# A four-image metaformer on one core: the scans' carried state multiplied into the factor by GpSimd, side work dealt by other weights, and the last token loads issued from ScalarE

## The chip, the core and the metric

The kernel runs on one core of a Trainium2 chip. The metric is the device time of one execution in microseconds (us). Before the change the median of three runs is 9317.89 us (9309.0 to 9324.41). One further execution was profiled; its own time is 9321.34 us, and its span in the trace is 9319.6 us.

## What is computed

The input x is four images of 64 x 64 tokens with 128 channels. Two layers follow each other, and each adds a mixing part and then a feed-forward part to x. In outline:

```
x  = x + ss2d(norm(x))            # in-projection, 3x3 depthwise convolution, four selective scans,
                                  # norm, gate, out-projection
t  = t + experts(norm(t))         # softmax over the 4096 tokens of an image for each of 64 experts,
                                  # the 8 best tokens of each expert pooled by their probabilities,
                                  # two dense layers, result added back to those tokens
x  = x + row_and_column_sums(norm(x))
t  = t + stu(norm(t))             # long convolutions with 16 filters by Fourier transform
```

The selective scan of the reference, for one image, one of four directions, and each of 256 channels d and 16 states n:

```
dA = exp(dt * A);   h = dA * h + (dt * u) * B;   y = sum over n of h * C     # one after the other over 4096 tokens
```

The expert part in the reference takes the softmax first and then picks its eight largest values:

```
probs = softmax(logits, axis=1); vals, idx = top_k(probs, 8)
pooled = sum(x[idx] * vals);  out = gelu([pooled, 1] @ weight1);  out = [out, 1] @ weight2;  outputs[idx] += out * vals
```

## The kernel before, in words

**The scan loop** (L2340 to L2479) makes up most of the program. An image is worked in 32 chunks: four directions k times eight pieces of 512 tokens. A chunk is worked in 16 steps, one for each state n, with the channels in two halves h of 128 partitions. Four images give 128 chunks and 2048 steps. In a step s the engines do this:

- SP (SyncE) issues the load of B and C for step s+5, spread over all partitions (tile bc, L2347).
- ScalarE computes da = exp(dl * aneg) for step s+3, 128x512 for each half (L2357). There are five da buffers.
- VectorE multiplies db = du * B for each half (L2414); du and db lie in PSUM. Then it runs the scan hh = da * h + db for each half with tensor_tensor_scan (L2420). The scan's initial value is the constant 0 in the first chunk of a direction (step == 0), and in the other seven chunks the state that the chunk before ended with, read from the tile hst: 1792 of the 2048 steps.
- GpSimd copies the last column of hh of step s-1 into hst (L2432, 128x2), and multiplies hh by C in place (L2433, 128x1024).
- TensorE transposes hh of step s-2 and adds it up in PSUM (L2460).

For directions 2 and 3 all of it runs from right to left.

**Waits taken early** (L2420 to L2423). The second scan of step s is given three dependencies ahead of need: on da of step s+1 (the dictionary acts), on GpSimd's multiplication of step s-7 and on TensorE's transposes of step s-7, since there are eight hh buffers (HH = 8).

**Chunk sizes** (step_sizes, L2233): in steps 1 to 10 of a chunk, dl and dx of the next chunk are made in pieces, among them two GpSimd operations of 128x1024 (L2271 and L2280). At step 15 ScalarE copies dx to du in PSUM (into_psum, L2337).

**Side work.** Everything else of the layers runs beside the scans as generators that yield a number after each piece of work, its supposed cost. Twice in each step the function deal takes pieces until their sum has caught up with what is due; what falls due at each call comes from the list WEIGHT (one total for each image, L41). Steps 2, 3 and 14 of a chunk deal nothing (BUSY). Dealt pieces stand in each engine's queue behind that step's own instructions. Helpers of the side work: norm_sums (L350: ScalarE makes sums and squares of four or two 128-wide rows), norm_refine (L369: six small GpSimd operations), norm_apply and transposed, pipelined (runs stages over groups, a cost for each stage).

**The experts of the first three images** (experts_and_sums, L1155) are side work. VectorE takes the maximum of each logit piece (L1197), ScalarE takes the exponentials (L1209) and scales them by one over their sum (L1219), VectorE picks the top eight of the probabilities (L1223) and blanks them (L1226), and GpSimd subtracts, so that only the eight values stay. Pooling and the two dense layers follow. The experts of the last image have their own function.

**After the scans**: the last image's experts and layer 1, then spectrum (L1930): 32 rounds of products on TensorE with copies alternating between VectorE and ScalarE. Its tile wt takes 128 KB of each partition. Each round sends its products to memory (zf), and the next round reads them back, transforms them (backward, L2044) and stores zd. Last comes endings (L2110): eight groups, for each of which zb (from zd) and the tokens x3 (tile xr) are loaded, four pairs of products are made, scaled and added to xr on VectorE (L2141), and xr is stored to out (L2145). All these loads and stores are issued by SP, in the order of the program.

Of the kernel before, what the change touches and what calls it, by code (L numbers as in the profile page):

```python
# [10 lines left out]
F32 = mybir.dt.float32  # L11
# [6 lines left out]
P = 128  # L18
# [22 lines left out]
WEIGHT = (1275.0, 1008.0, 1346.0, 927.0)  # L41
# [6 lines left out]
BP = 64  # L48
# [62 lines left out]
def kernel(  # L111
# [310 lines left out]
    def front(first_sizes):  # L422
# [6 lines left out]
        with tc.tile_pool(name="fr", bufs=2) as fr:  # L429
# [176 lines left out]
            for g in range(1, 8):  # L606
# [15 lines left out]
                for h in range(2):  # L622
                    if g == 1:
                        ps = cv[1][h]
                    else:
                        ps = bank([P, 8, W], "cv_ps")
                        for t in range(0, 9, 3):
                            taps_pe(ps, g, h, range(t, t + 3))
                            yield 2.6
# [57 lines left out]
    def before_scans(b):  # L687
# [6 lines left out]
        with tc.tile_pool(name="pa", bufs=1) as pa:  # L694
            xnT = pa.tile([P, L], F32, name="xnT")
            with tc.tile_pool(name="pa_n", bufs=2) as pn:
# [6 lines left out]
                def sums(g):  # L703
# [5 lines left out]
                    (3.0, sums),  # L709
                    (1.2, lambda g: norm_refine(pn, st[g], 4, C, 1e-6)),  # L710
                    None,
                    (1.2, lambda g: norm_apply(xt[g], xt[g], st[g], 4)),
                    None,
                    (1.0, lambda g: transposed(xnT[:, 512 * g : 512 * (g + 1)], xt[g], 4, "xt_ps")),
                )
            later(3, lambda: nc.sync.dma_start(xn_d[b], xnT))
            with tc.tile_pool(name="pa_c", bufs=2) as pc:
                for h in range(2):
# [17 lines left out]
                    for g in range(8):  # L736
                        ps = bank([P, 8, W], "cv_ps")
                        for t in range(9):
# [8 lines left out]
                            if t % 3 == 2:  # L747
                                yield 2.6
# [60 lines left out]
    def gate(b):  # L809

        z_d[b] = dram.tile([2, P, L], F32, name=f"z_d{b}")
        with tc.tile_pool(name="pa_z", bufs=2) as pz:
# [24 lines left out]
            yield from pipelined(16, (0.5, load), None, None, (2.8, project), (1.3, mul), (0.5, put))  # L837

    def after_scans(b, last=None):

        with ExitStack() as pools:
# [85 lines left out]
            if not last:  # L927
# [3 lines left out]
                    (2.2, add),  # L931
                    (2.0, sums),
                    (1.2, lambda g: norm_refine(po, st[g], 2, DI, 1e-5)),
                    None,
                    (1.2, apply),
                    None,
                    (1.0, turn),
                    (1.2, gated),
                    None,
                    (1.4, project),  # L940
# [65 lines left out]
    def filters():  # L1006

        with tc.tile_pool(name="fl", bufs=2) as fp:
# [45 lines left out]
            for src, acc in ((m_plus, accp), (m_minus, accm), (m_u, mu_t)):  # L1054
                n = src.shape[1]
                for i in range(4):
                    for k in range(0, n, 4):
# [10 lines left out]
                        yield 1.5  # L1068
            for k in range(0, KF, 4):
# [10 lines left out]
                yield 3.0  # L1080
# [11 lines left out]
        with tc.tile_pool(name="hd_w", bufs=2) as hp:  # L1092
# [41 lines left out]
            for q in range(0, NQ, 4):  # L1134
# [18 lines left out]
                yield 2.0  # L1153

    def experts_and_sums(b):  # L1155

        with tc.tile_pool(name="mk", bufs=1) as kp:
            pT = kp.tile([E, L], F32, name="pT")
            outE = kp.tile([E, C], F32, name="outE")
            pooled = kp.tile([P, E], F32, name="pooled")  # L1160
            with tc.tile_pool(name="ga", bufs=2) as gp:
                tt = gp.tile([P, NBLK, C], F32, name="tt", bufs=1)
                mx8 = gp.tile([E, 8], F32, name="mx8", bufs=1)
# [15 lines left out]
                def logits(g):  # L1179
# [7 lines left out]
                    (3.0, sums),  # L1187
                    (1.2, lambda g: norm_refine(gp, st[g], 4, C, 1e-5)),
                    None,
                    (1.2, lambda g: norm_apply(t4(g), t4(g), st[g], 4)),  # L1190
                    None,
                    (1.0, turn),
                    (1.0, logits),
                    None,
                    (
                        0.6,
                        lambda g: nc.vector.reduce_max(  # L1197
                            mx8[:, g : g + 1], pT[:, gs(g)], axis=AX.X
                        ),
                    ),  # L1200
                )
                yield LAG

                nmx = gp.tile([E, 1], F32, name="nmx", bufs=1)
# [1369 lines left out]
```

## Time and profile before

| what | us |
|---|---|
| median of three runs | 9317.89 |
| profiled execution, its time | 9321.34 |
| profiled execution, its span | 9319.6 |
| scan stage: from the first db to the end of the last scan | 48.0 to 7639.9 |
| last image's experts and layer 1 | to about 7877 |
| spectrum, 32 rounds | to about 9174 |
| rest of the last backward, and endings | to 9319.6 |

| engine | busy us | share of the span |
|---|---|---|
| TensorE (PE) | 7286.4 | 78% |
| VectorE (DVE) | 8204.7 | 88% |
| ScalarE (ACT) | 6078.9 | 65% |
| GpSimd (POOL) | 6345.1 | 68% |

GpSimd works almost only in the scan stage: its digits in the table of 40 slices are 6 to 9 until slice 33 and 0 in the last seven. A row of a group in the profile gives line, engine, operation, output and inputs with their shapes and the count; after the first bar the busy time in us and the mean of one in ns; after the second bar the idle time of the engine just before these instructions, with what ended most of it. A row of the waits gives who waited for whom, the sum in us, how often, and the longest. A row of the windows gives each engine's busy time in a stretch of the span, the clock granted to TensorE, the busy share of the DMA engines and their rate.

### The profile page before, as it was taken

What the parts mean: (1) busy time and instruction counts of PE and PEld (TensorE: products, weight loads), DVE (VectorE), ACT (ScalarE), POOL (GpSimd) and SP (SyncE); (2) the same over time, 40 slices, a digit from 0 to 9 for tenths busy, and PEclk for the clock granted to TensorE, in tenths of its full rate; (3) what the DMA queues carried; (4) which work ended last, traced back from release to release, by engine and by line L of the source; (5) the groups of instructions that cost most, each with busy time, mean ns of one, the idle gap of its engine ahead of it and who ended that gap; (6) DMA issues with size and microseconds to landing.
All of it is one profiled execution on the core that took longest, in us unless ns stands there. A gap on an engine that the chain in (4) does not pass through costs nothing.

```text
span 9319.6 us, 139792 instructions
## 1 busy us (share of the span) xinstructions
PE 7286.4 (78%) x45218; PEld 4705.1 (50%) x45218; DVE 8204.7 (88%) x9342; ACT 6078.9 (65%) x11459; POOL 6345.1 (68%) x5833
## 2 busy tenths in 40 slices
PE   7778787577777777787868777768777768999996
PEld 4445454355544555454544554544555445555663
DVE  8999999989999999999999999999999974556663
ACT  6676767657855576776875686875577763555552
POOL 6778788969888788877978798977888870000000
PEclk8889797668778888798878897868888878999998
DMA  5656657658566656657857656856756775333336
GB/s 167 214 194 205 210 185 250 202 187 253 188 201 222 221 174 198 207 185 235 254 178 245 223 174 220 260 171 238 239 179 209 218 224 171 96 90 94 95 95 181
DMA packets 918579, 1806.25 MB, mean 194 GB/s; under 512 B 86593, under 2 KB 476513, under 8 KB 914137
## 3 DMA queue, kind: packets, MB, share of 16 engines
q1 hardware_dynamic: 917848, 1797.30, 60.2%
q8 instruction: 363, 5.95, 0.3%
q14 instruction: 368, 3.01, 0.1%
HBM read 1554.75 MB, written 242.22 MB: 193 GB/s over the span
## 4 chain that ended last, share of the span: by engine, by line
POOL 34%; PE 24%; issue 15%; DVE 10%; ACT 8%; DMA 7%; SPq 1%; POOLq 0%; DVEq 0%; ACTq 0%
POOL hh L2433 26%; PE sp_ps L1944 10%; DVE hh L2420 5%; PE y L2460 4%; DVE wt L1948 3%; ACT da L2357 3%; DVE db L2414 2%; PE dl_ps L2277 2%; POOL hst L2432 2%; DMA bc<-bc_d 2%; POOL dx L2280 2%; POOL ex L2271 1%; DMA yk<-y_d 1%; ACT no_sq L362 1%; PE cv_ps L740 1%
## 5 line engine op out<-in xcount | busy, mean ns | idle before, releaser
L2433 POOL TENSOR_TENSOR hh<-hh,bc 128x1024 f32<-128x1024 f32 x2048 | 4830.9, 2360 | 330.2 <-DVE hh L2420 176.6
L2420 DVE TENSOR_TENSOR_SCAN hh<-da,hst,db 128x512 f32<-128x512 f32 x3584 | 4385.7, 1265 | 112.1 <-PE y L2460 61.7
L2460 PE MATMUL y<-ident,hh 128*128 128x128 f32 x16384 | 2623.4, 314 | 1094.1 <-POOL hh L2433 1005.2
L2357 ACT ACTIVATE da<-dl,aneg 128x512 f32<-128x512 f32 x4096 | 2776.6, 717 | 1054.5 <-DVE hh L2420 1042.2
L2460 PEld LDWEIGHTS y<-ident,hh 128*128 128x128 f32 x16384 | 2198.4, 162 | 1979.4 <-POOL hh L2433 1336.4
L2414 DVE TENSOR_TENSOR db<-du,bc 128x512 f32<-128x512 f32 x4096 | 2618.9, 684 | 151.6 <-ACT du L2337 107.9
L2432 POOL COPY hst<-hh 128x2 f32<-128x2 f32 x1792 | 336.8, 188 | 701.8 <-DVE hh L2420 628.4
L1948 DVE COPY wt<-sp_ps 128x1024 f32<-128x1024 f32 x512 | 606.6, 1221 | 168.6 <-PE sp_ps L1944 146.4
L1944 PE MATMUL sp_ps<-vt,pT_a 32*128 32x256 f32 x8192 | 592.6, 400 | 53.1 <-DVE wt L1948 32.8
L2420 DVE TENSOR_TENSOR_SCAN hh<-da,db 128x512 f32<-128x512 f32 x512 | 596.4, 1206 | 19.3 <-ACT no_r L366 9.9
L1948 ACT COPY wt<-sp_ps 128x1024 f32<-128x1024 f32 x512 | 515.4, 1016 | 121.5 <-PE sp_ps L1944 102.4
L1944 PEld LDWEIGHTS sp_ps<-vt,pT_a 32*128 32x128 f32 x8192 | 394.7, 185 | 246.9 <-DVE wt L1948 190.4
L1948 DVE COPY zs<-sp_ps 128x1024 f32<-128x1024 f32 x132 | 161.7, 1225 | 363.9 <-DMA gq<-dft_out 132.7
L1944 PE MATMUL sp_ps<-wt,ut 128*32 128x256 f32 x8192 | 450.3, 380 | 2.0 <-ACT ut L1948 2.0
L740 PE MATMUL cv_ps<-xh,diag 128*128 128x512 f32 x864 | 398.8, 597 | 4.4 <-ACT sg_v L409 3.1
L2277 PE MATMUL dl_ps<-ex,ident 128*128 128x512 f32 x508 | 308.7, 696 | 118.2 <-POOL ex L2271 113.6
L2252 PE MATMUL dt_ps<-dts,dtw 8*128 8x512 f32 x508 | 351.8, 798 | 49.1 <-ACT sg_v L409 24.1
L1944 PEld LDWEIGHTS sp_ps<-wt,ut 128*32 128x32 f32 x8192 | 263.6, 110 | 197.0 <-issue 25.2
L2280 POOL TENSOR_TENSOR dx<-dl,xc 128x1024 f32<-128x1024 f32 x127 | 300.3, 2365 | 89.9 <-ACT dl L2278 85.6
L2278 ACT COPY dl<-dl_ps 128x512 f32<-128x512 f32 x254 | 147.3, 580 | 324.6 <-PE dl_ps L2277 323.7
L1948 ACT COPY zs<-sp_ps 128x1024 f32<-128x1024 f32 x132 | 133.6, 1012 | 329.5 <-DMA zf<-zs 212.4
L2271 POOL TENSOR_TENSOR ex<-ex,dx 128x1024 f32<-128x1024 f32 x127 | 299.9, 2362 | 49.2 <-ACT dx L2268 40.0
(400 smaller groups left out, 9067.5 us busy)
## 6 DMA issues: line engine op xcount, KB each, us to landing
bc<-bc_d SPq DMA_DIRECT2D x2048, 512.0 KB
xc<-xc_d SPq DMA_DIRECT2D x128, 512.0 KB
y_d<-ys SPq DMA_DIRECT2D x128, 512.0 KB
w1t<-in_w_dram SPq DMA_DIRECT2D x96, 512.0 KB
w2t<-in_w_dram SPq DMA_DIRECT2D x192, 256.0 KB
yk<-y_d SPq DMA_DIRECT2D x128, 256.0 KB
yk<-y_d SPq DMA_DIRECT2D x256, 128.0 KB
zf<-zs SPq DMA_DIRECT2D x512, 64.0 KB
```

The costliest lines, as they stand in the source:

```text
L740: nc.tensor.matmul(ps, diag[:, h, t, :], xh[:, 8 * g + dy : 8 * g + dy + 8, dx : dx + W], start=(t == 0), stop=(t == 8),)
L1944: tc.keep_in_program_order(nc.tensor.matmul(*args, **kw))
L1948: tc.keep_in_program_order(copy(dst, src))
L2271: nc.gpsimd.tensor_sub(ex, ex, dx)
L2277: nc.tensor.matmul(ps, ident, t[:, h], start=t is dl, stop=t is w)
L2280: nc.gpsimd.tensor_mul(dx, dl, xc)
L2357: i_act = nc.scalar.activation(das[t][:, h, :], sizes[t // N][0][:, h, :], AF.Exp, scale=aneg[:, tk, h, t % N : t % N + 1],)
L2414: nc.vector.tensor_mul(db[h], dus[i][h], bcs[s][:, 0, :])
L2420: i_dve = nc.vector.tensor_tensor_scan(o, d0, d1, init, ALU.mult, ALU.add)
L2432: nc.gpsimd.tensor_copy(hsts[t // N][:, :, t % N], hhs[t][:, :, last])
L2433: i_pool = nc.gpsimd.tensor_mul(hhs[t], hhs[t], bcs.pop(t)[:, 1:2, :].to_broadcast([P, 2, SC]))
L2460: i_pe = nc.tensor.matmul(ys[c][:, q, h, :], hhs[t][:, h, q * P : (q + 1) * P], ident, is_transpose=True, start=(n == 0 and k > 0 and q % ...
```

## The change

There are four parts.

**1. The carried state.** In steps of chunks with step > 0, GpSimd multiplies the first-processed column of da by hst before the scan (two values in each partition, 128x2), and the scan starts from the constant 1. The multiplication for step s+2 stands in GpSimd's queue ahead of the copy and the multiplication of step s-1. It takes the place of the exponential in acts, so that the early wait of the second scan of step s is now for GpSimd's multiplication for step s+1.

```
+            t = s + 2
+            if 0 <= t < total and chunks[t // N][2] > 0:
+                col = SC - 1 if chunks[t // N][1] >= 2 else 0
+                d0 = das[t][:, :, col]
+                i_fold = nc.gpsimd.tensor_mul(d0, d0, hsts[t // N - 1][:, :, t % N])
+                acts[t] = i_fold.ins.name
...
-                    init = 0.0 if step == 0 else hsts[i][:, h, n : n + 1]
+                    init = 0.0 if step == 0 else 1.0
```

**2. Side work weighed anew.** The costs that the pieces yield are changed, and with them the totals. No work is added or removed by this; other pieces stand beside other steps.

```
-WEIGHT = (1275.0, 1008.0, 1346.0, 927.0)
+WEIGHT = (1494.0, 1288.0, 1692.0, 1196.0)
...
-                            yield 2.6
+                            yield 3.1
...
-                    (3.0, sums),
-                    (1.2, lambda g: norm_refine(pn, st[g], 4, C, 1e-6)),
+                    (5.4, sums),
+                    (2.2, lambda g: norm_refine(pn, st[g], 4, C, 1e-6)),
...
-                        yield 1.5
+                        yield 2.4
```

The first yield is that of three convolution taps; the last that of the filters (L1068). Nearly all stages of pipelined are changed in this way: those with norm_sums, norm_refine, norm_apply and GpSimd multiplications by factors of 1.2 to 2.3, the projections and expert products hardly or not.

**3. Raw top eight** (the experts of the first three images). The top eight are taken of the logits. The maximum is the first of them, the exponentials stay without their division, and the eight values get the same exponential, so that match_replace finds them. One over the sum is applied to the first dense layer's output, on the way out of PSUM, and to the second's.

```
-                        lambda g: nc.vector.reduce_max(
-                            mx8[:, g : g + 1], pT[:, gs(g)], axis=AX.X
-                        ),
...
+                nc.vector.max(top, pT)
...
-                nc.vector.reduce_max(nmx, mx8, axis=AX.X)
-                nc.vector.tensor_scalar(nmx, nmx, -1.0, None, ALU.mult)
+                nc.vector.tensor_scalar(nmx, top[:, 0:1], -1.0, None, ALU.mult)
...
+                nc.scalar.activation(top, top, AF.Exp, bias=nmx)
-                for g in range(8):
-                    nc.scalar.activation(pT[:, gs(g)], pT[:, gs(g)], AF.Identity, scale=ssum)
-                    yield 0.8
-                nc.vector.max(top, pT)
...
-                evict(h1, hps)
+                nc.scalar.activation(h1, hps, AF.Identity, scale=ssum)
...
+                nc.scalar.activation(outE, outE, AF.Identity, scale=ssum)
```

**4. The endings' tokens.** After the last product of spectrum, its tiles wt and zs and the pool that holds the taps are released, and all 32 token loads are issued on ScalarE's queue, ahead of the last read-back and the last backward. Two of the eight groups take the room of the older pool; the other six and zb take that of zs and wt. The copy of the last backward goes to VectorE. In endings SP issues zb and out alone.

```
+            right.close()
+            last_pool.__exit__(None, None, None)
+            begin_endings()
             load_back(n - 1)
             backward(n - 1)
...
-                out(zo, ps, 1)
+                out(zo, ps, 1 if i + 1 < n else 0)
...
+        for g in range(n):
+            for b in range(B):
+                nc.scalar.dma_start(xr[g][:, b], mine(x3_d, b, g))
...
-            def load_x(g):
-                xr[g] = gp.tile([P, B, 4, C], F32, name="xr3", bufs=6)
-                for b in range(B):
-                    nc.sync.dma_start(xr[g][:, b], mine(x3_d, b, g))
```

## The prediction

> **What bounds the kernel now.** I read the page's busy shares and slices first, then the groups of instructions, then the waits of the scan stage, then windows of the endings.
>
> ```profile
> PE 7286.4 (78%) x45218; PEld 4705.1 (50%) x45218; DVE 8204.7 (88%) x9342; ACT 6078.9 (65%) x11459; POOL 6345.1 (68%) x5833
> ...
> DVE  8999999989999999999999999999999974556663
> ...
> POOL 6778788969888788877978798977888870000000
> ```
>
> The second and third lines are the slices of VectorE and GpSimd. VectorE is at 9 tenths until slice 33, that is, through the whole scan stage of 7592 us (48.0 to 7639.9). The windows view gives VectorE 7304.6 us busy there, 96%, GpSimd 6298.4 us (83%), TensorE 76%, ScalarE 69%. So VectorE sets the pace, and what its instructions save is time, unless it then waits.
>
> ```profile
> L2433 POOL TENSOR_TENSOR hh<-hh,bc 128x1024 f32<-128x1024 f32 x2048 | 4830.9, 2360 | 330.2 <-DVE hh L2420 176.6 <-DMA dts_d<-xd_st 2.4 <-DMA bc<-bc_d 1.7
> L2420 DVE TENSOR_TENSOR_SCAN hh<-da,hst,db 128x512 f32<-128x512 f32 x3584 | 4385.7, 1265 | 112.1 <-PE y L2460 61.7 <-ACT da L2357 14.2 <-ACT vs L295 11.5
> ...
> L2420 DVE TENSOR_TENSOR_SCAN hh<-da,db 128x512 f32<-128x512 f32 x512 | 596.4, 1206 | 19.3 <-ACT no_r L366 9.9 <-ACT da L2357 5.7 <-PE y L2460 1.2
> ...
> L2432 POOL COPY hst<-hh 128x2 f32<-128x2 f32 x1792 | 336.8, 188 | 701.8 <-DVE hh L2420 628.4 <-PE y L2460 10.3 <-DMA bc<-bc_d 9.2
> ...
> L374 POOL TENSOR_TENSOR no_a<-no_a,no_r 128x2 f32<-128x2 f32 (+1 forms) x200 | 39.5, 197 | 31.0 <-ACT no_r L366 20.6
> ...
> L1197 DVE TENSOR_REDUCE mx<-pT 64x1 f32<-64x512 f32 x24 | 15.7, 654 | 0.0
> ```
>
> A step of VectorE is two db (684 ns) and two scans. The scans that read hst take 1265 ns, those with a constant 1206 ns, same shapes. From the records' starts, an undisturbed step lasts 3538 ns with hst and 3417 ns without. The rows behind L2432 and L374 are the price of 128x2 on GpSimd: 188 ns a copy, 197 ns a multiplication.
>
> ```profile
> DVE db L2414 <- ACT du L2337: 107.9, 65, 7.3
> DVE hh L2420 <- PE y L2460: 62.9, 35, 7.2
> ...
> DVE hh L2420 <- ACT da L2357: 20.0, 16, 3.2
> ```
>
> VectorE stands idle some 280 us of the stage. Of that 162 us end with ScalarE (107.9 for du, 20.0 for da, the rest five small rows), 63 us with TensorE's transposes, 40 us with the loads of bc. VectorE hardly ever waits for GpSimd directly today.
>
> **Scans from a constant.** 1792 steps are of the kind with hst. By the row means, 3584 x 59 ns = 211 us; by the step starts, 1792 x 121 ns = 217 us. I take 217: overlaps between instructions are in it, and the 256 steps without hst are the same instruction with a constant already. All of it is on the path.
>
> **The fold on GpSimd.** 1792 x 197 ns = 353 us busy. A GpSimd instruction that needs nothing of the one before starts about 60 ns before that one ends, so the queue grows by some 140 ns a step, 250 us. What hides it is GpSimd's waiting for scans, 805 us (rows hst 628.4 and hh 176.6). That cover is thin: copy 188, a gap of 80, multiplication 2360, less 55 of overlap is 2.57 us a step; side work on GpSimd in the stage is 1228 us, 0.60 a step; with the fold 3.31 us, against 3.42 of an undisturbed step of VectorE and some 3.6 with its idle time. Were the cover gone wholly, up to 250 us would come back; that is within the slower rival below.
>
> Here a rule speaks against the change. The Trainium skill, GPSIMD Engine Reference, section "Performance versus the Vector engine", keeps elementwise work on VectorE, because GpSimd dispatches each instruction through two software hops. The row agrees that it is dear: 197 ns for two columns. By the rule the fold would be VectorE's: with the form (N+151)/0.96 ns of VectorE: DVE Perf Modes (its section on the TRN2 errata) that is 159 ns, an estimate, x 1792 = 285 us on the engine that is the bound, 68 us more than the scans save. By the row it is 353 us on an engine with 805 us of waiting. I take the row; what the rule warns of is paid in the next term.
>
> **The new wait.** The second scan of step s now waits for the fold of s+1. In GpSimd's queue that stands behind the multiplication of s-3, and behind side work dealt in between; and it waits itself for da of s+1, with the copy and multiplication of s-2 queued behind it. Before, VectorE waited for the multiplication of s-7 only. The multiplication ends within 2.7 us of its scan's end in a quarter of the steps, 3.0 in half, 7.5 in 95 of 100, 19.8 at most. The second scan of step s starts 3 x 3.42 - 1.17 = 9.1 us after the scan of s-3 has ended. Less the usual 2.7 and the fold's 0.2, a burst of about 6 us on GpSimd is covered; by the same sum for s-7 some 20 us were.
>
> No trace of before shows the wait, so I count it from the records: where would the fold end, if it followed the multiplication of s-3 and its da, and is that behind the start of the second scan? In 67 of 2044 steps, in 23 bursts; within a burst one delay serves all, and the largest of each add up to 28 us. With a further lag of 1, 1.5, 2 or 3 us the same count gives 58, 78, 101 and 169 us. The lag does grow: in a burst GpSimd loses 0.14 us a step to the fold and 0.12 to the faster VectorE; over six steps 1.6 us. I take the row for 1.5 us, +78 us, with the ends +28 and +169. Below zero it can't go: the fold takes no wait away.
>
> **The weights.** In both programs the pieces of each image add up to its total within 1%, so nothing is left over for an image's end. What changes is the crowding. I sum the side instructions of each engine between the steps in the order of the two programs, each at the mean of its line's row. On GpSimd the largest sum in three consecutive steps falls from 14.9 to 8.7 us. On ScalarE the largest in 16 steps falls from 71.6 to 57.6 us, and the 99th percentile from 61 to 51, where the step's own two exponentials of 717 ns leave some 34 us (16 x (3.6 - 1.43)). The waits of VectorE that end with ScalarE, 162 us, come from such crowds; I take a quarter off, -40 us. Ends: -80 (half), and +20, since the convolution taps stand a few per cent closer than before. TensorE is what comes next there: in the stretches 150 to 430, 660 to 920, 1140 to 1420 and 4040 to 4320 it is 82 to 87% busy.
>
> **Raw top eight.** Row L1197: 24 maxima x 654 ns = 15.7 us leave VectorE, beside scans that follow without a gap: -16 us. MAX8 and MATCH_REPLACE8 (4.39 and 4.40 us each) stay. ScalarE loses 24 scalings of 710 ns (17 us) and gains six small ones; off the path, zero. If ScalarE were late there, it could only help.
>
> **Endings.**
>
> ```profile
> core 0: us, PE busy (x) PEld busy (x) DVE busy (x) ACT busy (x) POOL busy (x), PEclk, DMA share, GB/s
> ...
> 9174.00:9190.00 16.00, 5.81 (x8) 2.21 (x8) 0.00 (x0) 1.42 (x2) 0.00 (x0) 0.79 0.38 119
> 9190.00:9200.00 10.00, 0.00 (x0) 0.00 (x0) 0.00 (x0) 0.00 (x0) 0.00 (x0) 0.60 0.83 179
> 9200.00:9310.00 110.00, 68.29 (x121) 28.16 (x122) 21.78 (x29) 0.00 (x0) 0.00 (x0) 0.79 1.03 266
> ```
>
> After the last product the DMA engines are 38% busy for 16 us and 83% for 10 us, then full to the end. The empty part is 16 x 0.62 + 10 x 0.17 = 11.6 us. SP issues the first token load at 9191.8, behind the wait for zd; ScalarE's last copy ends at 9174.4, and from there it can issue. Everything after is transfer (8 MB each of zb, x3 and out), so filling the hole is worth 11 us. Behind the waiting ScalarE stands nothing; zq, zd and the first zb now share the engines with tokens, and the second half of the first zb waits for half of the token loads, but transfers run meanwhile. VectorE's copy of zo instead of ScalarE's is +0.2 us. Ends: 0 (if the read-back is delayed by as much) and -15.
>
> The rule here: DMA: Bandwidth & Descriptors of the Trainium skill, section "Issuing engines are not separate DMA queues", says that a second issuing engine saves only issue time. The token loads hold SP for 32 us of issuing (eight groups, 2.2 to 6.5 us), but under full DMA engines, so by the rule alone the gain would be nothing. By the windows the start moves 17 us earlier into a hole. I take the windows.
>
> **Sum.** -217 - 16 - 11 + 78 - 40 = -206 us, against the profiled execution's 9321.3: 9115 us. (The median of the runs is 3.4 us lower than that execution; too little to shift it.) The scan stage would take 7592 - 217 - 16 + 78 - 40 = 7397 us.
>
> **Rivals.**
>
> *The bound moves on.* VectorE is 3.4% faster, the others are not. In the four stretches where TensorE is 82 to 87% busy, some 1100 us or 300 steps, 121 ns a step (36 us) are not earned; the fold costs its upper end of 169, the weights bring nothing: 9321 - 244 + 36 + 169 = 9282 us; down to 9200 in milder forms. For it: VectorE's waits for TensorE lie just there. Against: TensorE's granted clock in them is 0.88 to 0.93, not full.
>
> *All of it arrives.* Waits at the lower end of 28, weights at -80: 9321 - 244 + 28 - 80 = 9025 us. For it: the thinner crowds are exactly what makes the fold late. Against: GpSimd at 3.31 of 3.42 us.
>
> *Slower: the fold holds GpSimd behind a late ScalarE.* The fold waits for da in order, ahead of a multiplication that could run. By the records da of s+2 ends after GpSimd could go on in 331 of 2044 steps, in sum 832 us. The gain is used up when 244 / 832 = 29% of that reaches VectorE. At 40% it is 333 - 244 = +89: 9410 us. Against it: in a burst the same lateness is counted in each step, GpSimd has 6 us in hand, and VectorE itself waited for da only 20.0 us in 16 places.
>
> **Chances.** The forecast (9050 to 9200) 0.67; the bound moves on (9200 to 9300) 0.18; all of it arrives (below 9050) 0.07; slower 0.08. A measurement of this kernel can tell about 0.2% (19 us) from no change. Of the second case 0.03 falls within that: faster 0.89, same 0.03, slower 0.08. The range 9050 to 9260 leaves out the third and fourth cases and some 0.04 of the second.
>
> **What would show it.** All 4096 scans at about 1206 ns, none with hst; 1792 multiplications da<-da,hst near 197 ns; a new wait of the scans for POOL da between 28 and 169 us; VectorE's waits ending with ScalarE nearer 120 than 162 us; L1197 gone; DMA engines over 90% busy from the last product on. I am wrong if the scans keep 1265 ns, if waits for POOL da pass 250 us, or if GpSimd's fold row has hundreds of us of idle time ended by ACT da.

## The result and the profile after

The changed kernel takes 9443.61 us (median of three runs, 9437.12 to 9450.17) against 9317.89: it is slower, ratio 1.0136 with a 95% interval of 1.0113 to 1.0159, or +126 us. The prediction of 9115 us was wrong in sign. The profiled execution has a span of 9448.4 us. Its scan stage lasts 7727.6 us (47.7 to 7775.3; before 7591.9), and what follows the stage 1673.1 (before 1679.7). So the loss lies in the scans.

First the busy shares and the slices of VectorE and GpSimd on the page after:

```profile
PE 7331.3 (78%) x45218; PEld 4741.4 (50%) x45218; DVE 7990.5 (85%) x9316; ACT 6070.9 (64%) x11441; POOL 6614.9 (70%) x7625
...
DVE  8898898889999999888989997999998983566553
...
POOL 7788888879988888887988897888888881000000
```

VectorE lost 214 us of work (8204.7 to 7990.5), where the sum had 217 + 16, and GpSimd gained 270. But VectorE's digits, 9 nearly throughout the stage before, are now often 8, in a longer stage: it does less and waits more. The groups of instructions say how much, and for what:

```profile
L2444 POOL TENSOR_TENSOR hh<-hh,bc 128x1024 f32<-128x1024 f32 x2048 | 4834.2, 2361 | 278.8 <-DVE hh L2431 130.4 <-DMA fr<-dft_in 3.2 <-DMA bc<-bc_d 1.3
L2431 DVE TENSOR_TENSOR_SCAN hh<-da,db 128x512 f32<-128x512 f32 x4096 | 4772.2, 1203 | 489.8 <-POOL da L2373 311.8 <-PE y L2471 162.5 <-PE xt_ps L395 5.3
...
L2373 POOL TENSOR_TENSOR da<-da,hst 128x2 f32<-128x2 f32 x1792 | 349.6, 200 | 155.8 <-ACT da L2361 137.8 <-DMA ud<-uo 4.6 <-DMA bc<-bc_d 3.0
...
L2443 POOL COPY hst<-hh 128x2 f32<-128x2 f32 x1792 | 339.7, 190 | 547.6 <-DVE hh L2431 492.4 <-PE y L2471 6.4 <-DMA bc<-bc_d 6.3
```

All 4096 scans take 1203 ns, and a fold takes 200 ns: both as forecast. New is the idle time ahead of the scans, 489.8 us where it was 131, and 311.8 us of it end with the fold (POOL da, L2373). The waits, for the lines that the prediction had shown:

```profile
DVE hh L2431 <- POOL da L2373: 311.8, 209, 5.5
...
DVE hh L2431 <- PE y L2471: 162.5, 65, 16.1
...
POOL da L2373 <- ACT da L2361: 137.8, 92, 5.8
...
DVE db L2425 <- ACT du L2341: 87.5, 35, 6.8
```

In the whole stage VectorE is idle for 638 us, where it was 287: +351. Its work in the stage fell by 215 us (7304.6 to 7089.3). The difference is 136 us, and by that the stage grew.

The endings, by windows that begin where the last product is nearly done:

```profile
9300.00:9310.00 10.00, 8.77 (x164) 5.02 (x156) 3.68 (x3) 3.04 (x3) 0.00 (x0) 1.00 0.41 81
9310.00:9320.00 10.00, 1.71 (x2) 0.84 (x3) 0.00 (x0) 0.00 (x0) 0.00 (x0) 0.67 0.87 271
9320.00:9330.00 10.00, 4.64 (x7) 1.40 (x5) 1.23 (x1) 0.00 (x0) 0.00 (x0) 0.67 0.85 264
9330.00:9340.00 10.00, 0.00 (x0) 0.00 (x0) 0.00 (x0) 0.00 (x0) 0.00 (x0) 0.50 0.83 252
9340.00:9350.00 10.00, 0.00 (x0) 0.00 (x0) 0.00 (x0) 0.00 (x0) 0.00 (x0) 0.50 1.01 238
```

The DMA engines (last but one column) stand at 0.83 to 0.87 right after the last product, where they were at 0.38 before. The hole is filled.

### The profile page after: what moved, and what is told of

Same layout as the page of the kernel before. It is cut to its first block, busy times and chain, and to the rows that moved or that the text cites. A ratio compares the mean times of both kernels' runs of the same rounds, so it can differ in the third digit from the quotient of the medians.

```text
span 9448.4 us, 141374 instructions
## 1 busy us (share of the span) xinstructions
PE 7331.3 (78%) x45218; PEld 4741.4 (50%) x45218; DVE 7990.5 (85%) x9316; ACT 6070.9 (64%) x11441; POOL 6614.9 (70%) x7625
## 4 chain that ended last, share of the span: by engine, by line
POOL 38%; PE 24%; issue 14%; DVE 8%; DMA 8%; ACT 7%; SPq 0%; POOLq 0%; DVEq 0%; ACTq 0%
POOL hh L2444 26%; PE sp_ps L1934 10%; PE y L2471 4%; DVE hh L2431 3%; DVE wt L1938 3%; DMA bc<-bc_d 3%; PE dl_ps L2281 2%; ACT da L2361 2%; POOL da L2373 2%; POOL hst L2443 2%; POOL ex L2275 2%; POOL dx L2284 2%; DVE db L2425 2%; PE cv_ps L740 1%; PE dt_ps L2256 1%
## 5 line engine op out<-in xcount | busy, mean ns | idle before, releaser
L2431 DVE TENSOR_TENSOR_SCAN hh<-da,db 128x512 f32<-128x512 f32 x4096 | 4772.2, 1203 | 489.8 <-POOL da L2373 311.8
L2471 PE MATMUL y<-ident,hh 128*128 128x128 f32 x16384 | 2656.8, 316 | 1201.6 <-POOL hh L2444 1105.4
L2471 PEld LDWEIGHTS y<-ident,hh 128*128 128x128 f32 x16384 | 2221.6, 164 | 2086.6 <-POOL hh L2444 1422.0
L2373 POOL TENSOR_TENSOR da<-da,hst 128x2 f32<-128x2 f32 x1792 | 349.6, 200 | 155.8 <-ACT da L2361 137.8
L869 PE MATMUL yk_ps<-yk,ident 128*128 128x512 f32 x512 | 282.6, 690 | 70.9 <-DMA yk<-y_d 50.0
```

What stands on the lines that cost most here:

```text
L2373: i_fold = nc.gpsimd.tensor_mul(d0, d0, hsts[t // N - 1][:, :, t % N])
L2431: i_dve = nc.vector.tensor_tensor_scan(o, d0, d1, init, ALU.mult, ALU.add)
L2471: i_pe = nc.tensor.matmul(ys[c][:, q, h, :], hhs[t][:, h, q * P : (q + 1) * P], ident, is_transpose=True, start=(n == 0 and k > 0 and q % ...
```

## Where the fold stands in GpSimd's queue

One stretch of the changed kernel's time line shows what a wait of the scans looks like. First GpSimd, then VectorE; columns are start, duration (us), engine, line, operation, and in brackets the idle time just before and what ended it.

```profile
3867.36 0.19 POOL L2443 COPY hst<-hh 128x2 f32<-128x2 f32 x1 [1.32 <-DVE hh L2431]
3867.63 2.35 POOL L2444 TENSOR_TENSOR hh<-hh,bc 128x1024 f32<-128x1024 f32 x1
3869.93 1.28 POOL L831 TENSOR_TENSOR sg_v<-sg_v,sg_e 128x512 f32<-128x512 f32 x1
3871.16 0.20 POOL L2373 TENSOR_TENSOR da<-da,hst 128x2 f32<-128x2 f32 x1
3872.68 0.19 POOL L2443 COPY hst<-hh 128x2 f32<-128x2 f32 x1 [1.32 <-DVE hh L2431]
3872.95 2.35 POOL L2444 TENSOR_TENSOR hh<-hh,bc 128x1024 f32<-128x1024 f32 x1
3875.26 0.35 POOL L2373 TENSOR_TENSOR da<-da,hst 128x2 f32<-128x2 f32 x2
```

```profile
3866.07 2.33 DVE L2431 TENSOR_TENSOR_SCAN hh<-da,db 128x512 f32<-128x512 f32 x2 [1.81 <-POOL da L2373]
3868.32 0.67 DVE L2425 TENSOR_TENSOR db<-du,bc 128x512 f32<-128x512 f32 x1
3871.39 1.22 DVE L2431 TENSOR_TENSOR_SCAN hh<-da,db 128x512 f32<-128x512 f32 x1 [2.40 <-POOL da L2373]
...
3875.49 1.22 DVE L2431 TENSOR_TENSOR_SCAN hh<-da,db 128x512 f32<-128x512 f32 x1 [0.57 <-POOL da L2373]
```

The first row of VectorE begins with the second scan of step 1006. It ends at 3867.3, and only then can GpSimd copy and multiply step 1006; side work follows (L831); then comes the fold for step 1008 at 3871.16, and only behind it VectorE starts the second scan of step 1007, at 3871.39. The next round is the same. Each engine waits for the other: GpSimd 1.32 us for the scan, VectorE 2.40 us for the fold. Both stand idle in each round; the two form a loop of one step, 5.3 and then 4.1 us around, where a free step takes 3.42.

In the text of the program the fold for step t is issued ahead of the copy of t-3, so that the last multiplication ahead of it is that of t-4; the description of the change tells this order. GpSimd's records have another. I take theirs for the order of the queue as it was built, before anything ran: it is read from one profiled execution, but another program repeats it nearly to the number (experiment 10), and an order asked for in the program moves it (experiments 12 to 14). Why the folds were put there no run shows. From GpSimd's records, in order of their starts, I counted for each fold which multiplication stands last ahead of it, and put the waits beside it:

| last multiplication ahead of the fold for t | folds | scans that waited | us |
|---|---|---|---|
| t-2 | 164 | 158 | 242.3 |
| t-3 | 297 | 32 | 43.5 |
| t-4 (as in the text) | 438 | 12 | 13.8 |
| t-5 or t-6 | 893 | 8 | 11.2 |

The folds of the first row are 9% of all and make 78% of the wait. I found this only after the tenth experiment; what follows is told in the order in which it was run.

## The experiments

Ratios are to the kernel before on the same chip, with 95% intervals; times are medians. The kernel before took 9325 to 9333 us beside them.

**1. The fold and the constant alone**, on the kernel before.

```
+            t = s + 2
+            if 0 <= t < total and chunks[t // N][2] > 0:
+                ...
+                i_fold = nc.gpsimd.tensor_mul(d0, d0, hsts[t // N - 1][:, :, t % N])
+                acts[t] = i_fold.ins.name
...
+                    init = 0.0 if step == 0 else 1.0
```

> The fold and the constant 1 alone, on the kernel before (its costs of side work, top eight and endings). Theory A, short queue: the scans' wait for the fold follows from GpSimd's queue alone, so it is here too; waits for POOL da near 300 us, the wait for PE y near 63 us as before, time 9318 - 217 + 300 = about 9400 us, between 9370 and 9430. Theory B, crowding: the new costs of side work make GpSimd and TensorE late, and the fold alone is what I forecast; waits for POOL da under 150 us and 9318 - 217 + 78 = about 9180 us, up to 9250.

Measured: 9490.7 us, 1.0169 (1.0154 to 1.0184).

```profile
DVE hh L2427 <- POOL da L2369: 351.1, 228, 8.4
```

The fold by itself loses as much as the whole change or more (the intervals overlap). Theory B falls. Theory A has the wait for the fold roughly right (near 300), but its time was too low (9370 to 9430): the wait for PE y rose too (116.5 us).

**2. All but the fold**: the fold's lines left out, and the initial value again from hst.

> The changed kernel without the fold: scans read the kept state again; new costs, raw top eight and new endings stay. Theory A: it is faster than the kernel before by the top eight (16) and the endings (7), with or without something from the costs: 9260 to 9300 us. Theory B: the new costs do harm by themselves; the wait for PE y stays near 160 us and the time is 9318 + 100 - 23 = about 9395 us.

Measured: 9317.44 us, 0.9987 (0.998 to 0.9994). The rest of the change is a small gain and no harm. The wait for PE y is 97.7 us here.

**3. Each scan waits for its own fold**: one line less than the changed kernel.

```
-                acts[t] = i_fold.ins.name
```

> The changed kernel, but the second scan of step s does not wait for the fold of step s+1 ahead of need; each scan waits for its own step's fold, one step (3.4 us) later. Theory A, short queue: bursts of GpSimd up to about 9 instead of 6 us are covered, so the wait for POOL da falls from 312 to about 150 us and the time by as much: about 9290 us. Theory C, rate: GpSimd is at 3.3 of 3.4 us a step and cannot catch up, so that a step more of distance is used up at once: wait within 250 to 312 us, time above 9380 us. Theory D, ScalarE's lateness held in GpSimd's queue: the fold still stands ahead of the copy and the multiplication, idle time of GpSimd by ACT da stays at 138 us, and at least half of the wait for the fold stays: about 9370 us.

Measured: 9300.48 us, 0.9969 (0.9957 to 0.9981).

```profile
POOL da L2373 <- ACT da L2361: 144.6, 95, 5.8
...
DVE hh L2430 <- POOL da L2373: 94.3, 88, 5.4
```

The wait moves from the second scan of step s-1 to the first of step s. By the records that is some 2.3 us (a scan and two db), not the 3.4 that my expectation says. These 2.3 us take 217 us off the wait for the fold, and 0.0167 of before, 156 us, off the time. VectorE waits longer for other things instead: 117.8 us for du, 73.4 for bc. Theory A comes out in the time (about 9290), though the wait fell further than it said (150). Theory C falls, and so does D: GpSimd still waits 144.6 us for da, but less than a third of the wait for the fold is left.

**4. The costs of before** in the changed kernel (its totals WEIGHT counted anew).

> The changed kernel with the costs of the kernel before (totals counted anew for the pieces that the raw top eight leaves: 1275, 997, 1335, 916). Theory A: the fold's wait hardly depends on the costs; 9400 to 9470 us and POOL da at 270 to 350 us, while PE y falls from 162 toward 63 us. Theory B: waits for POOL da under 150 us and PE y near 63 us, time about 9180 to 9250 us.

Measured: 9491.58 us, 1.0171 (1.0156 to 1.0186); POOL da 337.7 us, PE y 122.6. Beside the fold the new costs save about 0.35%, 33 us, with an interval of some 25. The wait for the fold is where theory A had it, the time some 20 us above its range. It also equals the first experiment, though it has the top eight and the endings besides: those bring nothing beside the fold.

**5 to 7. The fold taken apart.** Three kernels with the constant 1, which leave out the state carried from chunk to chunk: nothing in the fold's place; a product of the same size written in its place (hst by hst, into a spare tile); and that product reading da's column.

```
+                h0 = hsts[t // N - 1][:, :, t % N]
+                nc.gpsimd.tensor_mul(spare, h0, h0)
```

```
+                nc.gpsimd.tensor_mul(spare, d0, hsts[t // N - 1][:, :, t % N])
```

> The changed kernel without the fold, its scans starting from the constant 1 (left out: the state carried from one chunk to the next). It is what the shorter scans are worth with neither load nor wait. By my prediction's first term: 9317 (the run with kept state and all else of the change) - 217 = 9100 us, up to 9115. If other engines already bind at this pace (the bound moves on), less of it arrives: 9150 to 9230 us, with VectorE's waits for PE y, du and bc above their sum of 240 us in the run with kept state.

> As the kernel with the constant 1 and no fold, and GpSimd multiplies the kept state by itself into a spare tile in the fold's place in its queue: the load of the fold, without waiting for da and without VectorE waiting for it (left out: the carried state). Theory A, short queue: the load alone costs little, within 40 us of the kernel without it, since GpSimd keeps a distance of seven steps. Theory C, rate: the load alone, 1792 x 200 = 358 us busy on an engine at 97%, brings back most of it: 9230 to 9300 us, through PE y and du rather than through a wait for POOL da.

> As the kernel with the load alone, but the spare product reads da's column, so that GpSimd waits in order for the exponential as the fold does, and VectorE still waits for nothing of it (left out: the carried state). Theory D, ScalarE's lateness held in GpSimd's queue: 100 us or more above the kernel with the load alone, with about 140 us of GpSimd's idle time by ACT da. Theories A and C: within 30 us of it.

Measured: 9184.11 us, 0.9841 (0.9827 to 0.9856), with nothing; 9250.18, 0.9912 (0.9895 to 0.9928), with the load; 9293.05, 0.9961 (0.9946 to 0.9976), with the wait for da.

With nothing in its place the shorter scans are worth 0.0146 of before (0.9987 to 0.9841), 136 us and not 217. The other 81 us are idle time of VectorE: 388 us in the stage against 306 in experiment 2. Its waits for PE y, du and bc are 306 us together, above the 240 that I had named as the sign of other engines binding. The waits of the three kernels, first with nothing:

```profile
DVE hh L2424 <- PE y L2464: 133.8, 49, 16.0
...
DVE db L2418 <- ACT du L2341: 104.8, 48, 9.9
```

then with the product of hst by hst:

```profile
DVE hh L2430 <- PE y L2470: 140.9, 54, 16.6
DVE db L2424 <- ACT du L2342: 136.9, 60, 10.3
```

then with the product that reads da:

```profile
DVE db L2425 <- ACT du L2342: 156.7, 64, 10.1
POOL spare L2374 <- ACT da L2362: 151.6, 103, 5.7
...
DVE hh L2431 <- PE y L2471: 127.3, 52, 16.6
```

The first product costs 66 us, and reading da 46 more. Hardly any of it shows as a wait for the product (19 us in three waits in experiment 7); du comes later (104.8, then 136.9, then 156.7). So the cover did not hide the load: theory C has the time of experiment 6 (9230 to 9300), and A, with 40 us at most, falls.

The 66 and the 46 are not cleanly load and waiting, though. "In its place" holds for the text alone: by GpSimd's records 1791 of the 1792 products of experiment 6 stand behind the multiplication of t-16, of the same state one chunk before, where hst has just been written. With da's column to read they stand where the fold stands (162, 299, 439 and 892 in the four places). So the 46 us hold the move to these places as well as the waiting for da (151.6 us of GpSimd), and a load in the fold's places that waits for nothing was not measured. The two together, 112 us, are what a fold costs that no scan waits for. Theory D, which asked for 100 or more for the waiting, and A and C, which allowed 30, all miss. Experiment 3 is within the intervals of 7: a scan that waits for its own fold pays nothing more that can be measured.

**8. The fold on VectorE**, ahead of the step's db, as the rule on elementwise work would have it.

```
+                if step > 0:
+                    d0 = das[s][:, :, SC - 1 if k >= 2 else 0]
+                    nc.vector.tensor_mul(d0, d0, hsts[i - 1][:, :, n])
```

> The changed kernel with the fold on VectorE, in its own stream just ahead of the step's two db; no engine waits for it. The nearest row of VectorE is a multiplication of 128x4 at 162 ns; x 1792 = 290 us on the path: 9317 - 217 + 290 = 9390 us if the rule's form holds, from 9340 (if half of a small instruction overlaps its neighbours) to 9400. All theories expect the wait for POOL da to be gone; it tells whether the rule would have been the better choice than the early wait (9443 us) and than the wait in its own step (9300 us).

Measured: 9814.77 us, 1.052 (1.0504 to 1.0536). The group of the fold:

```profile
L2419 DVE TENSOR_TENSOR da<-da,hst 128x2 f32<-128x2 f32 x1792 | 844.9, 485 | 117.7 <-ACT da L2361 117.1
```

485 ns for two columns. By the records 846 of these began while no GpSimd instruction ran, and took 134 ns; 946 began beside one and took 798. Those with 1.5 us or more of it still to go (180) took 1761; from 0.23 us to go upward they ended, in the median, 19 ns after the GpSimd instruction. The time is over 400 us above the upper end of what I expected (9400).

**9. The fold on ScalarE**, two activations of one column behind the step's exponentials.

> The changed kernel with the fold on ScalarE, two activations of one column right behind the step's two exponentials; GpSimd gets no load and VectorE waits for nothing new. Small activations of 128x2 take 198 ns in the kernel before: 3584 x 0.2 = 710 us more busy on an engine with some 30% of the stage free. If that is hidden, the time is that of the kernel with the constant 1 and no fold, 0.984 of before (about 9180 us); if ScalarE's crowds grow by it, VectorE's waits for du and da (140 us together with no fold) double, 9280 to 9330 us.

Measured: 9343.75 us, 1.0018 (1.0011 to 1.0025). GpSimd has no load, and nobody waits for it.

```profile
L2371 ACT ACTIVATE da<-da,hst 128x1 f32<-128x1 f32 x3584 | 883.9, 289 | 0.8
```

289 ns each and not 200. VectorE's waits for ScalarE grow to 257 us (127.0 du, 129.9 da in two rows), from 141 with nothing in the fold's place. They do not quite double, and still the time lies above both of my ranges.

**10. The fold's text one step earlier** (t = s + 3), early wait as in the change.

> The changed kernel with GpSimd's fold one step earlier in its queue (for step s+3, just behind the exponential's issue, instead of s+2), with the early wait as it is. The wait gains 3.4 us of distance, while GpSimd waits longer in order for da. Theory A, short queue: the wait for POOL da falls from 312 to under 100 us and the time from 9443 to about 9300 us, as it did when each scan waited in its own step (2.2 us of distance). Theory D, ScalarE's lateness held: GpSimd's idle time by ACT da at least doubles from 138 us and the time stays above 9400 us.

Measured: 9449.87 us, 1.013 (1.0115 to 1.0145); POOL da 313.9 us, ACT da 141.3: no different from the changed kernel. Both theories miss. Its folds stand in GpSimd's queue where they stood before (164, 297, 435 and 896 in the four places of the table): a step earlier in the text moved next to nothing. This is what made me look at the built queue.

**11. The load beside the slower scans**: the product of experiment 6, but scans from hst. It stands behind the multiplication of t-16 here too.

> The load of the fold (kept state times itself into a spare tile, on GpSimd) with the scans reading the kept state as before, so that VectorE goes at 3.54 instead of 3.42 us a step. Nothing is left out. With the constant 1 this load cost 66 us (9184 to 9250). Theory C, rate: GpSimd's 3.3 us a step hurt less at the slower pace, 10 to 35 us above the 0.9987 of before that the kernel without the load has. If the load costs by its place in the queue whatever the pace, it is 60 us or more.

Measured: 9367.09 us, 1.0046 (1.0031 to 1.006): 0.0059 above experiment 2, 55 us. At VectorE's slower pace the same load costs nearly what it costs at the faster (66). That is above the 10 to 35 us of theory C, though the intervals (some 20 us) leave its upper end open.

**12 to 14. The place held fast.** GpSimd's copy and multiplication of step s-1 are ordered behind the fold for s+2, which is an order within one queue: with the early wait; with each scan waiting in its own step; and with the fold for s+3.

```
+                        tc.add_manual_dep(i_copy.ins, i_fold.ins.name, order, reason="queued behind")
...
+                    tc.add_manual_dep(i_pool.ins, i_fold.ins.name, order, reason="queued behind")
```

> The changed kernel, early wait and all, with one thing more: in GpSimd's queue the copy and the multiplication of step s-1 are ordered behind the fold for step s+2, as the program's text has it. In the records of the changed kernel the compiled queue had put 164 of the 1792 folds behind the multiplication of the step just before the one whose scan waits (242 of the 311 us of waits), 297 one step, 438 two and 892 three steps further back (44, 14 and 11 us). Theory E, place in the queue: with all folds of the last two kinds (1786 of 1792) the wait for POOL da falls to 25 to 60 us and the time to 9290 to 9330 us, since the load (66) and the waiting in order for da (46) stay. Theory A, the short distance itself: the wait only moves to the other folds, over 200 us, and the time stays above 9390 us.

> The same order in GpSimd's queue, and each scan waits for its own step's fold instead of the second scan of the step before. Theory E: 78 of the 95 us of this wait stood behind folds in the nearest place; it falls below 20 us, and the time is 9230 to 9300 us, at the level of the kernel whose spare product nobody waits for (0.996 of before) or a little below. If it stays at 95 us or more, the place in the queue is not the cause.

> The order in GpSimd's queue one step earlier: the copy and the multiplication of step s-1 stand behind the fold for step s+3, early wait as in the change. Theory E: no wait for POOL da is left (under 20 us), but GpSimd waits longer in order for the exponential, which was issued just before: its idle time by ACT da goes from 138 to 250 us or more. Net between 9280 and 9380 us. If the time equals that of the order for step s+2 within 20 us, neither matters any more.

Measured: 9313.39 us, 0.9979 (0.997 to 0.9989), early wait; 9299.88, 0.9968 (0.9957 to 0.9979), own step; 9573.38, 1.026 (1.0243 to 1.0276), s+3. The waits of the first:

```profile
POOL da L2374 <- ACT da L2361: 231.9, 151, 5.8
...
DVE hh L2432 <- POOL da L2374: 143.9, 116, 6.3
```

and of the third:

```profile
POOL da L2374 <- ACT da L2361: 458.0, 260, 8.0
...
DVE db L2426 <- ACT du L2341: 198.2, 59, 8.5
DVE hh L2432 <- POOL da L2374: 194.6, 145, 4.7
```

Only 4 folds are left in the two near places in the first kernel, and it is 0.0157 of before, 146 us, faster than the changed kernel with the same load, the same wait and the same instructions. That shows that the place made the larger part of the wait's loss, though not alone. It made it together with the early wait: experiments 3 and 13, where each scan waits for its own fold, have the near and the far places (166 and 295 in the two nearest, against 0 and 4) and the same time, 0.9969 and 0.9968. Either one taken away, the 146 to 156 us are gone.

The wait for the fold falls by 168 us to 144, not to 25 to 60: an early place makes GpSimd wait longer in order for da (138 to 232 us), and folds at t-4 wait more than they did (125.9 us in 108 scans). The third kernel shows where this leads: with the fold ahead of everything GpSimd stands 458 us for ScalarE, and VectorE pays for it in all its waits. My "no wait left" for it was wrong, and its time lies some 190 us above my range. The second kernel, with 29 us of waits for the fold (I had expected under 20), is no faster than experiment 3: what remains then lies elsewhere.

**15. The second operand out of SBUF**: experiment 8 with two columns of du, in PSUM, for the kept state.

> As the kernel with the fold on VectorE (9815 us, 485 ns a fold), but the second operand is two columns of du, which lie in PSUM, instead of the kept state in SBUF (changed: the column is multiplied by du instead of by the carried state). In the records of that run the 846 folds that began while no GpSimd instruction ran took 134 ns, the 946 others 798 ns, and as long as the GpSimd instruction still had to go. If two operands in SBUF make VectorE wait for GpSimd, it takes 130 to 200 ns now and the time is 9184 + 1792 x 0.13 to 0.2 = 9415 to 9540 us. If the small size or the place in the stream made it slow, it stays near 485 ns and 9800 us.

Measured: 9274.27 us, 0.9937 (0.9922 to 0.9952).

```profile
L2419 DVE TENSOR_TENSOR da<-da,du 128x2 f32<-128x2 f32 x1792 | 252.9, 141 | 119.2 <-ACT du L2341 119.2
```

141 ns, and 240 at most: 139 in the 620 that began while no GpSimd instruction ran, 142 in the 1172 that began beside one. So it was the second operand in SBUF that made VectorE wait while GpSimd ran. In time it costs still less: an undisturbed step goes from 3.417 to 3.483 us, 66 ns; half of the small instruction lies under its neighbours. In all it costs 90 us over experiment 5 (0.9841), less than the 230 that I had put as the least.

**16. The top eight and the endings alone**, with the costs of before.

> The raw top eight and the new endings alone: the costs of side work of the kernel before and no fold. Against the kernel without the fold but with the new costs (0.9987 of before, scan stage 7593 against 7592 us) it weighs the costs by themselves. By my prediction's terms the top eight is worth 16 and the endings 7 as measured in the changed kernel: 0.9975 of before, scan stage 7576 us; the new costs then cost 15 us instead of saving 40. If the costs saved something, this kernel is at or above 0.9987.

Measured: 9333.35 us, 1.0003 (0.9994 to 1.0012). The two parts bring nothing that can be measured, and the new costs (experiment 2 against this) about 0.0016, 15 us, at the edge of the intervals. VectorE's work in the stage is 13 us less than before and its idle time 33 more (321 us), in a profiled execution that took 15 us longer: the 16 us of maxima are gone from its work and spent waiting.

## Why the prediction was wrong

The ladder in fractions of before, with each step in us:

| step | ratio after it | us |
|---|---|---|
| costs, top eight, endings (exp. 2) | 0.9987 | -12 |
| scans from a constant (5) | 0.9841 | -136 |
| GpSimd's load, behind the multiplication of t-16 (6) | 0.9912 | +66 |
| the load in the fold's places, waiting there for da (7) | 0.9961 | +46 |
| VectorE waits early, fold in its place (12) | 0.9979 | +17 |
| the fold's places in the built queue beside the early wait (the change) | 1.0136 | +146 |
| sum | | +127 |

Each step has an interval of some 0.0015 to 0.0025 of its own, 15 to 25 us, so the 17 may be nothing; experiment 12 also holds more waiting for da than 7, which would be in its step. In another order the steps could have other sizes (the load costs 55 us beside the slower scans).

The sum of the prediction was -206 us, the ladder's is +127: 333 us apart. Of these 112 are the fold's load and its waiting for da, which stood in the sum with nothing; 85 the new wait (17 + 146 instead of 78); 81 the scans (-136 instead of -217); 55 the weights, top eight and endings (-12 instead of -67). With the wait at its +78 the other measured terms still give +42, so the sign does not hang on the wait alone.

- **Two steps failed: the new wait and the load.** In *The new wait* it is "In GpSimd's queue that stands behind the multiplication of s-3". That is the order of the text. In the built queue 461 of the 1792 folds stand behind that of s-2 or s-1, and those made 286 of the 311 us of waits. Everything built on it fell with it: the "burst of about 6 us" that is covered is none where the fold waits for the scan just before; and "within a burst one delay serves all" does not hold in a loop of two engines, where each turn pays again (158 waits of 1.5 us in the nearest place). The +78 is 312 us of waits in the profile. In time it is 163 us, which lies just inside the upper end of 169; that is luck, since this end was made for a lag in the place s-3. The records of the kernel before could not show where the fold would stand; reading it from the changed program as built, before a run, was not tried.
- **The load**, in *The fold on GpSimd*, was counted at nothing, because 805 us of GpSimd's waiting for scans were to hide it. It cost 66 us, and 55 at the slower pace, where it stood one chunk ahead; in the fold's places and with the waiting for da it cost 112, the largest of the four misses. From experiment 5 to 6 GpSimd's waiting for scans falls by 132 us, so part of the load is hidden; but VectorE's idle time grows by 58 us, 32 of them for du. A waiting GpSimd is no free time where the added work delays what others need. By which path du comes later I can't say.
- **Scans from a constant**: the mechanism was right (1203 ns, 3.417 us a step), the size was not. Of 217 us, 136 arrive. "All of it is on the path" failed. The rest is the rival *The bound moves on*, which had put it at 36 us: of the 81 us of further idle time, some 70 are longer waits for PE y, du, bc and da than in experiment 2.
- **The weights**: forecast -40, measured about -15 without the fold and -33 with it; inside the ends. The mechanism is there: VectorE's waits in the stage that end with ScalarE are 193 us in experiment 16 and 128 in experiment 2, which differ in the costs alone. But the wait for PE y rises at the same time, from 67 to 98, and bc by 12; these take most of it back.
- **Raw top eight, -16**: L1197 is gone, but nothing of it arrives (experiments 4 and 16).
- **Endings, -11**: the windows show the filled hole, at 0.83 to 0.87 instead of over 0.9. After the scans the changed kernel needs 6.6 us less; over the profiles of all kernels with the new endings the mean is about 4 us less than before, and they scatter by 14.
- **The slower rival** came within 34 us of the time and was right in sign, by the wrong mechanism. The waiting for a late da in order is real, but costs some 46 us in experiment 7, the move of place included, and not 333 (with the early wait and the fold held a step earlier it costs more: experiment 14); GpSimd's idle time by ACT da is 137.8 us, not "hundreds". Of the three signs named in the prediction, it was the wait for POOL da over 250 us that came.
- **The rule on elementwise work**: I weighed 197 ns on GpSimd against an estimate of 159 ns on VectorE. Neither price decided. The Trainium skill, SBUF — State Buffer, section "Who interferes with whom", says that a VectorE instruction with two inputs in SBUF contends with a GpSimd instruction that reads SBUF, and that the later one is blocked. The runs agree: 798 ns beside one, 134 without, 141 with one operand in PSUM. With it in mind VectorE would have been ruled out for a better reason: 9815 us. The trace of before held the sign as well, in a multiplication of two SBUF tiles after the scans (durations in ns: least, median, longest):

```profile
L1779 DVE TENSOR_TENSOR a_l<-a_l,r_l x16: 161/163/3449, 7793.0 to 7864.2; 128x4 f32<-128x4 f32 x16
```

The one of 3449 ns began beside a long GpSimd copy (L1745) and ended 13 ns after it; no GpSimd instruction ran beside the other fifteen.

The fastest kernels that compute all of the reference are experiments 3 and 13, 0.9969 and 0.9968 of before: the change with one line less, without and with the order in the queue. They beat the kernel before by some 30 us and the changed one by some 155. A kept state in PSUM, folded by VectorE, would by experiment 15 be some 30 us better still before its own cost of getting there; it wasn't tried.

## What to carry to other kernels

Before a small cross-engine operation is put into a loop, find out which instruction stands ahead of it in its queue as built, or take it from a first trace; the place in the text is a wish, and one step too near, with an early wait on it, turns slack into a loop in which both engines wait for each other. A wait that is "taken early" is safe only while the thing waited for is early too. And take a cost apart on the chip in the order load, in-order wait, wait of others: each was paid here, and VectorE's waits name only the last. See where each stand-in stands in the queue, too: the one of experiment 6 stood a chunk away from what it stood for.

## What the runs showed of the hardware

A VectorE multiplication of 128x2 with both operands in SBUF takes 134 ns while GpSimd runs nothing. Beside a GpSimd instruction that has 0.23 us or more to go it ends some 19 ns after that one (485 ns in the mean of all, 485 x 1792 = 869 us in sum). With one operand in PSUM it takes 141 ns, GpSimd or not, and lengthens the stream by 66. A ScalarE activation of a single column with a scale from SBUF takes 289 ns in experiment 9. A GpSimd multiplication of 128x2 takes 196 ns (experiment 6) to 200 (the change), from hst alone or from da and hst.
